# Attention and a dequantized feed-forward layer on one core: the first and last microseconds rearranged, and the turning of the probabilities moved one unit further ahead

## The chip, the cores and the metric

The kernel runs on one core of one Trainium2 chip. The metric is the device time in microseconds (us); three runs give a median of 1543.86 (1541.33 to 1545.67). TensorE is written PE here, VectorE DVE, ScalarE ACT, GpSimd POOL and SyncE SP.

## The reference

x has 16 sequences of 256 tokens and 256 features, all in 32-bit floats. Two sub-layers follow, each with a layer norm (no weights) ahead of it and another behind it, and a residual sum:

```python
q = einsum('bpd,hde->bphe', x, W_Q) + b_Q          # 16 heads of 128; k and v likewise
scores = einsum('bqhe,bkhe->bhqk', q, k) / sqrt(128)
scores = where(causal, scores, -100000.0)
z = einsum('bkhe,bhqk->bqhe', v, softmax(scores))
attn = einsum('bqhe,hed->bqd', z, W_O) + b_O
...
gate, up = xt @ Wg.T, xt @ Wu.T                     # 2048 columns, from 4-bit codes and scales per 32
ffn = (gelu_tanh(gate) * up) @ Wd.T
...
x = x + layernorm(attn(layernorm(x)))
x = x + layernorm(ffn(layernorm(x)))
```

## The kernel before

**Precision.** A 32-bit operand is split into a high part and a rest, and a product is three passes of PE (`mm3`, line 353): high times high, low times high, high times low. Nearly everything outside PE turns results into such pairs: ACT writes the high part out of PSUM, DVE or POOL subtracts it to get the low part.

**Order of work.** The program is one long list. `run` (line 95, issuing in line 99, which is why nearly every row of the profile says L99) records each operation behind the last one of its engine, and `dma` (line 86, rows L88 and L91) does the same for SP, which issues all DMAs. So each engine works in the order in which Python calls these. Background work (layer norms, weight splits, dequantizing) is a generator in a lane (`urgent`, `behind`, `splits`, `idle`, `made`, `spare`); `slot(kinds, ...)` lets one lane take one step at a fixed place of the list.

**Attention.** The 4096 tokens are 8 blocks of 512 (two sequences). A *unit* is one block and one head, 128 in all; a *pair* is two heads, 64 in all. One pass i of the main loop (from -4 to N + 1) does, on PE in this order:

- `st_s(i + 3)`: scores of a unit; DVE adds the mask and finds the row minima, ACT takes exponentials and row sums, POOL multiplies by the reciprocals (tile pr);
- `st_qk(i + 4)`: keys (pk) and queries (pq) of the unit after it, ACT and DVE make kh, kl, kr and qh, ql, qr;
- `st_o(p - 1, i % 2)`: half of a pair's output projection (po);
- `st_z(i)`: probabilities times v (pz), then zh on ACT and zl on DVE;
- `st_v(i + 4)`: a quarter of the v product (pv) of two pairs.

The probabilities have to be turned: DVE transposes 32x32 blocks (`st_t(i + 3)`: tr), four DMAs write them to DRAM (`st_w(i + 3)`: hop<-tr), one reads them back rearranged in the next pass (`st_b(i + 2)`: pt<-hop, two buffers), and a pass later ACT and POOL split them (`st_p(i + 1)`: ph, pl). SP gets, at the end of a pass, first st_b, then st_w, then the weights.

**Weights.** In the first block each pair's weights are loaded raw, split (`w_split`) and kept in DRAM; later blocks load them back (`w_get`). `weights` asks for wk and wq of pair p + 4 in odd passes, and for wo of pair p and wv of pair p + 4 in even ones. Each of wk, wq, wv, wo has two buffers. At a block's end `mid` turns the projection through DRAM (ohop), adds and normalizes, and turns the tokens again (xhop), while `ln1` prepares the next block.

**Feed-forward weights** are dequantized meanwhile in 24 pieces (`f_make` on DVE, then `f_scale` on POOL and ACT), from the last pair of the first block on; small tiles (sg, t, v: tag "code") rotate over four buffers. `f_load` fetches a piece's codes and scales (ld).

**Feed-forward part.** 4 superblocks of two blocks, each with 8 groups of 256 columns: `Two` computes gate and up with seven products instead of eight (m1 to m7, tiles pa, pf, pe, pd), DVE and ACT combine them into `inter`, and `st_d` multiplies by wd one group later, into four PSUM banks that hold 512 tokens by 128 features each. At the end of a superblock the result is turned through DRAM (`end`); in the last one it is turned by PE (`end_now`).

**Ends.** `first_tokens` normalizes the first block: two pieces by DVE, two by ACT, with w_split(0, "k") and w_split(0, "q") between; eight transposes by PE (tpx) follow, behind 24 transposes of the identity that do no work (`warm`). `end_now` takes a block of 512 tokens: eight transposes (tpo), layer norm statistics of four pieces, two pieces normalized by ACT and two by DVE (fa), a residual sum for each half and the store.

Of the kernel before, what the change touches and what calls it, by code (L numbers as in the profile page):

```python
# [18 lines left out]
P = 128  # L19
# [3 lines left out]
NG = 8  # L23
# [5 lines left out]
def kernel(  # L29
# [215 lines left out]
    def first_tokens():  # L245

        xs = [x_load(x, 0, hf) for hf in range(2)]
        yield V_
        stats = []
        for hf in range(2):  # L250
            stats.append((yield from ln_stats([xs[hf][:, t, :] for t in range(2)])))
        w_split(0, "k")
        xn = wide("xn")
        nb = ln_shift(*stats[1], 2)
        for t in range(2):
            mv, rs = stats[0]
            run(
                nc.vector.tensor_scalar,
                xn[:, t, :], xs[0][:, t, :], mv[:, t, 0:1], rs[:, t : t + 1], ALU.subtract, ALU.mult,
            )  # L260
        for t in range(2):
            ln_apply_act(xn[:, 2 + t, :], xs[1][:, t, :], nb, stats[1][1], t)
        w_split(0, "q")
        xt = XT[1, 0] = work.tile([P, 2, 2, TB], F32R, tag="xT", name="xT", bufs=4)
        for hf in range(2):
            tp = ps.tile([P, 2, S], F32, tag=("pk", "pq")[hf], name="tpx")
            for kt in range(2):
                for t in range(2):
                    run(
                        nc.tensor.transpose,  # L270
                        tp[:, kt, t * P : (t + 1) * P], xn[:, 2 * hf + t, kt * P : (kt + 1) * P], ident,
                    )
            cols = slice(hf * S, (hf + 1) * S)
            hi, lo = xt[:, 0, :, cols], xt[:, 1, :, cols]
            run(nc.scalar.copy, hi, tp)
            run(nc.vector.tensor_tensor, lo, tp, f(hi), ALU.subtract)
        ready.add((1, 0))
# [20 lines left out]
    def w_split(p, n):  # L298
# [14 lines left out]
        if n in "vo":  # L313
            run(nc.gpsimd.tensor_tensor, wv_[:, 1], raw, f(wv_[:, 0]), ALU.subtract)
        else:
            run(nc.vector.scalar_tensor_tensor, wv_[:, 1], raw, c, f(wv_[:, 0]), ALU.mult, ALU.subtract)
# [36 lines left out]
    def mm3(o, terms, passes=STATIONARY_LAST, start=True, stop=True, shared=False):  # L353

        todo = [(lhs(a), rhs(c)) for lhs, rhs in terms for a, c in passes]
        for i, (lhs, rhs) in enumerate(todo):
            run(
                nc.tensor.matmul, o, lhs, rhs, start=start and i == 0, stop=stop and i == len(todo) - 1, skip_group_check=shared
            )
# [9 lines left out]
    def st_qk(i):  # L369
# [9 lines left out]
        mm3(pk, [(lambda a, kt=kt: wk_[:, a, kt, cols], lambda c, kt=kt: xt[:, c, kt, :]) for kt in range(2)], MOVING_LAST)  # L379
# [10 lines left out]
        mm3(pq, [(lambda a, kt=kt: wq_[:, a, kt, cols], lambda c, kt=kt: xt[:, c, kt, :]) for kt in range(2)], MOVING_LAST)  # L390
# [83 lines left out]
    def st_b(u):  # L474

        pt = work.tile([P, 4, 6, 32], F32, tag="pt", name="pt")
# [111 lines left out]
    LD = {}  # L588

# [8 lines left out]
    def f_make(g, n, then):  # L598
# [4 lines left out]
        def small_tile(dtype, name):  # L603
            return work.tile([P, 2, 256], dtype, tag="code", name=name, bufs=4)

        c = work.tile([P, 2, 256], I32, tag="raw", name="codes", bufs=6)
        sg, t, v = small_tile(BF16, "sg"), small_tile(BF16, "t"), small_tile(BF16, "v")
# [10 lines left out]
        yield V_  # L618
        run(nc.vector.scalar_tensor_tensor, v, c, 0.5, t, ALU.mult, ALU.max)
# [3 lines left out]
        run(nc.vector.scalar_tensor_tensor, v, sg, 1.0, v, ALU.add, ALU.mult)  # L623
        add(made, f_scale(g, n, v, sc), G_)

    def f_scale(g, n, v, sc):
        scb = sc.unsqueeze(1).to_broadcast([P, 2, 256])
        if n == "d":
            full = work.tile([P, 2, 256], F32, tag="raw", name="full", bufs=6)
            w = f_tile(n)  # L630
            run(nc.gpsimd.tensor_tensor, full, v, scb, ALU.mult)
            yield A_
            run(nc.scalar.copy, w[:, 0], full)
            run(nc.gpsimd.tensor_tensor, w[:, 1], full, f(w[:, 0]), ALU.subtract)
        else:

            full = work.tile([P, 8, P], F32, tag="eight", name="full", bufs=1)
            run(nc.gpsimd.tensor_tensor, full[:, 0:4].rearrange("p (k c) n -> p k (c n)", k=2), v, scb, ALU.mult)
            w = f_tile("u")
# [210 lines left out]
    def st_d(k, bb, dh):  # L850
# [17 lines left out]
        if g == NG - 1:  # L868
            if sb < NSB - 1:
                if dh == 0:  # L870
                    ACC[b] = back_tile()
                back(ACC[b], dh, po)
                if dh == 1:
                    add((urgent, behind)[bb], end(b, ACC.pop(b)), N_)
            else:
                if dh == 0:
                    ACC[b] = wide("oT").rearrange("p a b -> p (a b)").rearrange("p (h n) -> p h n", h=2)
                run(nc.scalar.copy, ACC[b][:, dh], po)
                if dh == 1:
                    add(urgent, end_now(b, ACC.pop(b), tags), V_)  # L880
# [16 lines left out]
    def end_now(b, oT, tags):  # L897

        yield V_
        tp = []  # L900
        for hf in range(2):
            tp.append(ps.tile([P, 2, D], F32, tag=tags[hf], name="tpo"))
            for t in range(2):
                for dh in range(2):
                    run(
                        nc.tensor.transpose,
                        tp[hf][:, t, dh * P : (dh + 1) * P], oT[:, dh, (2 * hf + t) * P : (2 * hf + t + 1) * P], ident,
                    )
        o = [tp[t // 2][:, t % 2, :] for t in range(4)]
        mv, rs = yield from ln_stats(o)  # L910
        nb = ln_shift(mv, rs, 4)
        fa = wide("fa")
        for t in range(2):
            ln_apply_act(fa[:, t, :], o[t], nb, rs, t)
        for t in range(2, 4):
            run(
                nc.vector.tensor_scalar,
                fa[:, t, :], o[t], mv[:, t, 0:1], rs[:, t : t + 1], ALU.subtract, ALU.mult,
            )
        for hf in (1, 0):  # L920
            run(nc.vector.tensor_tensor, X1[b][hf], X1[b][hf], fa[:, 2 * hf : 2 * hf + 2, :], ALU.add)
            dma(half(out, b, hf), X1[b][hf])
# [14 lines left out]
    for n in range(24):  # L937
        run(nc.tensor.transpose, warm[:, n % 4, :], ident, ident)
# [13 lines left out]
    for i in range(-4, N + 2):  # L952
        p = i // 2
        odd = i % 2 == 1
        if p >= 0 and not odd and p < len(pairs):
# [3 lines left out]
            if b == 0 and g == 7:  # L959
                pieces = [(fg, n) for fg in range(NG) for n in "gud"]  # L960
                f_load(*pieces[0])
                for m, piece in enumerate(pieces):
# [3 lines left out]
        if 0 <= i + 3 < N:  # L966
            st_s(i + 3)
        slot(V_)
        if i + 4 < N:
            st_qk(i + 4)  # L970
# [3 lines left out]
        if 0 <= i + 3 < N:  # L974
            st_t(i + 3)
# [6 lines left out]
        if i + 4 < N:  # L982
# [3 lines left out]
        if 0 <= i + 2 < N:  # L986
            st_b(i + 2)
        if 0 <= i + 3 < N:
            st_w(i + 3)
        if odd:  # L990
            weights((p + 4, "k"), (p + 4, "q"))
        else:
            weights((p, "o"), (p + 4, "v"))
# [14 lines left out]
    for k in range(NGRP + 1):  # L1008
        sb, g = divmod(k, NG)
        if k < NGRP:  # L1010
            if g == 2 and sb + 1 < NSB:
                while not {(0, 2 * sb + 2), (0, 2 * sb + 3)} <= ready:
                    step(behind)
                add(spare, x_ops(sb + 1), N_)
            if g == NG - 1:
                for b in (2 * sb, 2 * sb + 1):
                    X1[b] = [x_load(x1d, b, hf, ("pr", "tr")[b % 2]) for hf in range(2)]
# [15 lines left out]
        parts(k, "m7", "m3")  # L1033
        st_d(k - 1, 0, 0)
        slot(V_)
        slot(A_ + G_)
        parts(k, "m4")
# [3 lines left out]
    finish(urgent)  # L1041

# [50 lines left out]
```

## Time and profile before

| | us |
|---|---|
| median of three runs | 1543.86 (1541.33 to 1545.67) |
| the profiled execution | 1548.52 |
| its span, first to last instruction | 1546.7 |
| PE busy | 1510.8 (98%) |
| DVE busy | 1178.4 (76%) |
| ACT busy | 1033.0 (67%) |
| POOL busy | 810.1 (52%) |
| DMA, mean | 263 GB/s |

A row of the timeline has the start, the length, the engine, the line, the operation, the tiles (written <- read) and the number of instructions in it; brackets give the idle time before it and what ended that. Matmuls are pipelined and their ends are modelled, so for PE the distance between starts is read, not the length. SPq is SP issuing DMAs. A row of the windows view has the stretch, its length, then for PE, PE's weight loads, DVE, ACT and POOL the busy us and the instructions, then the granted PE clock, the busy share of the DMA engines and GB/s. The chain is the work that ended last, each step followed back to what released it.

### The profile page before, as it was taken

The page shows a single profiled execution, that of the slowest core. Times are in us where ns is not written, and L with a number is a line of the kernel's source. Part 1 is how long each engine was busy: PE and PEld are TensorE (multiplying, and loading weights), DVE is VectorE, ACT ScalarE, POOL GpSimd, SP SyncE. Part 2 cuts the span into 40 slices and gives each one's busy share as a digit, 9 for nine tenths or more (in the row PEclk, how much of TensorE's full clock was granted, in tenths as well). Part 3 has the DMA queues.
Part 4 walks back from the last instruction along what each step waited for, and adds up shares of the span by engine and source line. Part 5 has one row for each costly group of instructions (what it writes and reads, how often), then busy time and mean ns, then how long its engine had stood idle before and what let it go on. Part 6 is the DMA issues. An engine that isn't in the chain of part 4 may idle for free.

```text
span 1546.7 us, 25648 instructions
## 1 busy us (share of the span) xinstructions
PE 1510.8 (98%) x7792; PEld 1281.4 (83%) x7792; DVE 1178.4 (76%) x2944; ACT 1033.0 (67%) x2600; POOL 810.1 (52%) x1017
## 2 busy tenths in 40 slices
PE   8999999999999999999999999989999999999996
PEld 7888888888888888888888888877788878878884
DVE  6875878788788788878777777847777777787765
ACT  6876667767767676676675777656666665665663
POOL 3754669568667767766866866861420330240100
PEclk9999999999999999999999999989999999999999
DMA  8998899989899999899899889975547456655551
GB/s 276 335 310 257 249 303 302 313 293 300 280 293 317 291 310 296 267 326 309 266 315 294 287 281 322 324 238 204 216 179 275 185 220 212 236 192 214 218 195 42
DMA packets 200411, 407.55 MB, mean 263 GB/s; under 512 B 21457, under 2 KB 128465, under 8 KB 189521
## 3 DMA queue, kind: packets, MB, share of 16 engines
q1 hardware_dynamic: 200272, 405.91, 78.6%
q8 instruction: 62, 1.02, 0.3%
q14 instruction: 77, 0.62, 0.1%
HBM read 294.15 MB, written 111.67 MB: 262 GB/s over the span
## 4 chain that ended last, share of the span: by engine, by line
PE 80%; DMA 6%; DVE 5%; ACT 4%; SPq 2%; issue 1%; POOL 0%; DVEq 0%; POOLq 0%; ACTq 0%
PE pd L99 11%; PE po L99 10%; PE pk L99 10%; PE pv L99 10%; PE pq L99 9%; PE pz L99 9%; PE sc L99 8%; PE pa L99 7%; PE pf L99 5%; DVE sum L99 3%; DMA wo<-wo 2%; PE pe L99 2%; SPq L91 2%; ACT inter L99 1%; DMA hop<-tr 1%
## 5 line engine op out<-in xcount | busy, mean ns | idle before, releaser
L99 POOL TENSOR_SCALAR pr<-pr,rc 128x128 f32<-128x128 f32 (+1 forms) x512 | 251.7, 508 | 80.8 <-DVE rc L99 80.8
L99 POOL TENSOR_TENSOR pl<-pt,ph 128x512 fp32r<-128x512 f32 x128 | 165.3, 1291 | 218.3 <-ACT ph L99 211.8
L99 ACT ACTIVATE pr<-sc,mn 128x128 f32<-128x128 f32 (+1 forms) x512 | 208.9, 421 | 83.1 <-DVE mn L99 81.7
L99 DVE CUSTOM_DVE_ANT_0 sc<-sc,mask 128x128 f32<-128x128 f32 (+1 forms) x512 | 180.7, 373 | 63.5 <-PE sc L99 54.7
L99 PE MATMUL pv<-wv,xT 128*128 128x512 f32 x768 | 208.9, 407 | 0.0
L99 PE MATMUL pd<-inter,wd 128*128 128x512 f32 x768 | 199.5, 393 | 5.2 <-ACT inter L99 4.0
L99 PE MATMUL pk<-xT,wk 128*128 128x512 f32 x768 | 201.5, 398 | 1.6 <-ACT wv L99 1.4
L99 PE MATMUL pq<-xT,wq 128*128 128x512 f32 x768 | 196.4, 391 | 0.0
L99 ACT ACTIVATE zh<-pz,bqk 128x512 fp32r<-128x512 f32 x128 | 88.5, 692 | 160.6 <-PE pz L99 160.6
L99 POOL TENSOR_TENSOR rs<-rs,mhalf 128x4 f32<-128x4 f32 (+1 forms) x33 | 35.1, 1065 | 288.5 <-DVE rs L99 287.2
L99 PEld LDWEIGHTS pd<-inter,wd 128*128 128x128 f32 x768 | 142.3, 188 | 42.5 <-DVE inter L99 7.0
L99 PEld LDWEIGHTS pq<-xT,wq 128*128 128x128 f32 x768 | 144.5, 188 | 32.9
L99 PE MATMUL po<-zh,wo 128*128 128x512 f32 x512 | 160.3, 394 | 8.4 <-DMA wo<-wo 8.4
L99 PEld LDWEIGHTS pk<-xT,wk 128*128 128x128 f32 x768 | 136.5, 190 | 25.5 <-ACT xT L99 1.6
L99 PEld LDWEIGHTS pv<-wv,xT 128*128 128x128 f32 x768 | 135.0, 189 | 23.6
L99 DVE SCALAR_TENSOR_TENSOR zl<-pz,bqk,zh 128x512 fp32r<-128x512 f32 x128 | 95.2, 744 | 76.9 <-ACT zh L99 76.7
L99 ACT COPY part<-pa 128x512 f32<-128x512 f32 x192 | 111.9, 586 | 62.4 <-PE pa L99 59.8
L99 ACT CAST inter<-sum 128x512 fp32r<-128x512 f32 x128 | 80.1, 626 | 101.1 <-DVE sum L99 100.9
L99 DVE TENSOR_TENSOR inter<-sum,inter 128x512 fp32r<-128x512 f32 x128 | 92.1, 720 | 58.9 <-ACT inter L99 56.0
L99 DVE STREAM_TRANSPOSE tr<-pr 128x768 f32<-128x768 f32 x128 | 123.3, 963 | 1.1
L99 PEld LDWEIGHTS po<-zh,wo 128*128 128x128 f32 x512 | 96.1, 189 | 31.1 <-DMA wo<-wo 11.5
L99 DVE SCALAR_TENSOR_TENSOR kl<-pk,bqk,kh 128x512 fp32r<-128x512 f32 x128 | 96.0, 750 | 30.3 <-ACT kr L99 27.1
(139 smaller groups left out, 3792.6 us busy)
## 6 DMA issues: line engine op xcount, KB each, us to landing
hop<-tr SPq DMA_DIRECT2D x512, 96.0 KB
pt<-hop SPq DMA_DIRECT2D x128, 384.0 KB
wk<-wk SPq DMA_DIRECT2D x64, 512.0 KB
wq<-wq SPq DMA_DIRECT2D x64, 512.0 KB
wo<-wo SPq DMA_DIRECT2D x64, 512.0 KB
wu<-fu SPq DMA_DIRECT2D x32, 1024.0 KB
wg<-fg SPq DMA_DIRECT2D x32, 1024.0 KB
wv<-wv SPq DMA_DIRECT2D x56, 512.0 KB
```

The lines of the kernel that those rows point to most:

```text
L91: queue[0] = nc.sync.dma_start(dst, src).ins
L99: ins = op(dst, *args, **kw)
```

## The change

Six things are done at once.

1. *First tokens.* DVE normalizes all four pieces; w_split(0, "k") comes after them and w_split(0, "q") after the copies of the turned tokens. The idle transposes are 30 instead of 24, with 3 and 6 more behind the two groups of tpx. The first v weights' low part goes from POOL to DVE.
2. *Order of passes in pk and pq* (`lows_last`): both high parts of the tokens first, their low parts last.
3. *One unit further ahead.* Scores, keys, turning and its store and load (`st_s`, `st_qk`, `st_t`, `st_w`, `st_b`) are called with an index one higher, the loop begins at -5, and pt has three buffers. `st_p`, `st_z`, `st_o` and `st_v` keep their index.
4. *Weights.* wk and wq are asked for in even passes; wo of pair p + 1 and wv of pair p + 5 in odd ones, which is one pass earlier for these two.
5. *Dequantizing.* The first `f_load` comes at pair 6 instead of 7, two passes earlier; `code` has three buffers, and before v is allocated the scaling of the piece before must stand in the list (`unscaled`).
6. *Last tokens.* The last group's m4 comes ahead of st_d(k - 1, 0, 0). `end_now` is gone; `st_last` takes the last group of the last superblock in four halves of 256 tokens: matmuls of 256 columns, copy, transposes, statistics, and the residual in one step of DVE and one of ACT, one half behind the other. The last half is stored in two pieces.

```diff
@@ first_tokens
-        w_split(0, "k")
         xn = wide("xn")
-        nb = ln_shift(*stats[1], 2)
-        for t in range(2):
-            mv, rs = stats[0]
+        for t in range(4):
+            mv, rs = stats[t // 2]
             run(
                 nc.vector.tensor_scalar,
-                xn[:, t, :], xs[0][:, t, :], mv[:, t, 0:1], rs[:, t : t + 1], ALU.subtract, ALU.mult,
+                xn[:, t, :], xs[t // 2][:, t % 2, :], mv[:, t % 2, 0:1], rs[:, t % 2 : t % 2 + 1],
+                ALU.subtract, ALU.mult,
             )
-        for t in range(2):
-            ln_apply_act(xn[:, 2 + t, :], xs[1][:, t, :], nb, stats[1][1], t)
-        w_split(0, "q")
+        w_split(0, "k")
...
+            keep_warm(3 + 3 * hf)
...
+        w_split(0, "q")
         ready.add((1, 0))
@@ mm3
+        if lows_last:
+            todo = [todo[m] for m in (0, 1, 3, 4, 2, 5)]
@@ st_b
-        pt = work.tile([P, 4, 6, 32], F32, tag="pt", name="pt")
+        pt = work.tile([P, 4, 6, 32], F32, tag="pt", name="pt", bufs=3)
@@ f_make
-            return work.tile([P, 2, 256], dtype, tag="code", name=name, bufs=4)
+            return work.tile([P, 2, 256], dtype, tag="code", name=name, bufs=3)
...
+        while unscaled:
+            step(made)
+        v = small_tile(BF16, "v")
         run(nc.vector.scalar_tensor_tensor, v, c, 0.5, t, ALU.mult, ALU.max)
@@ main loop
-    for i in range(-4, N + 2):
+    for i in range(-5, N + 2):
...
-            if b == 0 and g == 7:
+            if b == 0 and g == 6:
                 pieces = [(fg, n) for fg in range(NG) for n in "gud"]
                 f_load(*pieces[0])
+            if b == 0 and g == 7:
...
-        if 0 <= i + 3 < N:
-            st_s(i + 3)
+        if 0 <= i + 4 < N:
+            st_s(i + 4)
         slot(V_)
-        if i + 4 < N:
-            st_qk(i + 4)
+        if i + 5 < N:
+            st_qk(i + 5)
...
-        if 0 <= i + 2 < N:
-            st_b(i + 2)
         if 0 <= i + 3 < N:
-            st_w(i + 3)
+            st_b(i + 3)
+        if 0 <= i + 4 < N:
+            st_w(i + 4)
         if odd:
+            weights((p + 1, "o"), (p + 5, "v"))
+        else:
             weights((p + 4, "k"), (p + 4, "q"))
-        else:
-            weights((p, "o"), (p + 4, "v"))
@@ st_last, in place of end_now
+        count = len(halves)
+        for n in range(count + 2):
+            if n < count:
+                multiply(n, 0)
+            if 0 <= n - 1 < count:
+                turn_and_measure(n - 1)
+            if n < count:
+                multiply(n, 1)
+            if n >= 2:
+                apply(n - 2)
```

In `apply`, DVE computes x1 + o * rs and ACT adds the shift nb to it:

```python
run(nc.vector.scalar_tensor_tensor, x1[:, t, :], os[n][t], rs[:, t : t + 1], x1[:, t, :], ALU.mult, ALU.add)
run(nc.scalar.activation, x1[:, t, :], x1[:, t, :], AF.Identity, bias=nb[:, t : t + 1])
```

## The prediction, made before the run

> **What bounds the kernel now.** I read the page's busy times first, then the list of what TensorE (PE) waited for, then the chain in order of time, then timelines around each wait. The profiled execution took 1548.52 us, 1546.7 of it span and 1.8 around it. The median of the three runs is 1543.86, so the profiled one is 4.7 slow. About 0.3% (4.6 us) is what a measurement of this kernel can tell from no change.
>
> ```profile
> PE   8999999999999999999999999989999999999996
> ...
> PEclk9999999999999999999999999989999999999999
> ```
>
> The first row is PE's busy share in 40 slices, the second its granted clock, both in tenths: full in nearly every slice; only the two ends and the 27th slice of PE (where attention gives way to the feed-forward part) show anything. So nothing is to be had from shorter work on other engines, only from PE's gaps. In the middle one unit of attention costs a constant: the chain names the first key matmul (pk) at 369.55 and 377.38, 7.83 us apart, and so on for most of 128 units. Where the spacing is larger, PE lost the difference.
>
> ```profile
> 825.63 1.40 PE pk L99 x6
> 835.30 2.43 POOL pr L99 x4
> 839.97 6.26 DMA wo<-wo
> 846.27 2.64 PE po L99 x6
> ...
> 853.19 1.40 PE pk L99 x6
> ```
>
> Three units should pass in 23.50 us between 825.63 and 853.19; they took 27.56. The chain leaves PE for a load of wo that was issued at 839.97 and landed at 846.23. The waits of PE name the same culprit:
>
> ```profile
> PE po L99 <- DMA wo<-wo: 8.4, 6, 4.1
> PE pd L99 <- ACT inter L99: 4.0, 4, 1.9
> PE sc L99 <- DVE kl L99: 2.3, 1, 2.3
> ```
>
> The columns are us in total, times, longest. The DMA queue's own timeline says why wo was late: SP issues everything in order, and at a block's boundary it stood for the read back of the turned output.
>
> ```profile
> 835.59 0.34 SPq L91 DMA_DIRECT2D o<-ohop  x1
> ...
> 837.57 0.42 SPq L91 DMA_DIRECT2D pt<-hop  x1
> 838.09 1.84 SPq L91 DMA_DIRECT2D hop<-tr  x4
> 839.97 0.46 SPq L91 DMA_DIRECT2D wo<-wo  x1
> ```
>
> A long gap costs twice. In windows of 3.4 us the granted clock falls to half afterwards (the figure after the busy times):
>
> ```profile
> 10.40:13.80 3.40, 2.93 (x7) 2.38 (x8) 0.92 (x2) 1.00 (x2) 2.51 (x2) 0.50 0.98 374
> ...
> 153.80:157.10 3.30, 3.30 (x11) 2.91 (x12) 2.96 (x11) 0.97 (x5) 2.05 (x2) 0.50 0.46 99
> ...
> 846.70:850.10 3.40, 3.40 (x13) 2.92 (x12) 3.40 (x11) 2.30 (x8) 3.32 (x8) 0.50 0.94 278
> ```
>
> **Part 1, the wo load one unit earlier.** It moves from the end of unit 2p to the end of unit 2p-1; its reader, the output projection, stays. Pieces: pk spacings over 7.83 at wo waits are 1.04 + 0.17 (from 211), 0.58 (353), 1.08 and 0.58 (589, 606) and 4.06 (841), together 7.5 us, half clock included. Each of these waits is under 2.4 us and the new lead is 7.83 more, so all go: **-7.5**. The load now also waits for the previous reader of its buffer, a projection that PE starts 1.4 us before it is done; SP reaches it later anyway (a projection at about 836.2 to 837.6, the wo issue at 839.97). Queued behind it on SP are the v half, then the next pt load; the v half waits for the unit's last v matmul, about 840.0, against an issue at 840.47, so nothing. What is late next: the k and q loads, which trade places with wo and v and now stand behind the boundary's copies. Such a load, issued at 839.97 and landing at 846.23, is first needed three units after unit 2p began (824.6 + 23.5 + 1.15 of scores = 849.2): 3 us of cover.
>
> **Part 2, scores, turning and storing one unit ahead, three pt buffers.** In the steady state PE's order is the same, with other unit numbers; scores still stand one unit behind their keys. pt gets a unit more between its store and its use. It held ScalarE 37 us over 20 times, but no row of PE's waits names pt, so in the middle I cost it at 0; without that cover the bound is -0.7 (at 845 the pt product was due about when PE would have asked for it). At the drain it counts. From the last scores at 1016.60 to the end of the last projection (1042.88 + 2.75 = 1045.63) PE took 29.0 us for: scores 1.15, six projections of 1.36, four pz of 1.09, three feed-forward products of 1.36, together 17.8. So 11.3 are lost, to a wo wait of 4.08 behind hop<-tr, a pz wait of 1.49, and the half clock from 1024.2 to 1027.5 and from 1031.0 to 1037.7. After, the last scores come one unit before this, pz and pv lie behind them, and no hop<-tr stands just before the last wo. What stays is one short turn: pz 1.07, zh 0.6, ph 0.6, pl 1.29 and 0.3 of handovers are 3.9 to the next pz, with 2.45 of PE work in it: 1.2 to 1.8 lost, and perhaps 1.7 for a half clock. I take 3 left: **-8.3** (between -5 and -10).
>
> **Part 3, the first load of feed-forward weights two units earlier.**
>
> ```profile
> 144.89 0.44 SPq L91 DMA_DIRECT2D ld<-in_gp  x1
> ...
> 151.73 0.49 DVE L99 TENSOR_SCALAR codes<-ld 128x256 int32<-128x256 int32 x2 [5.90 <-DMA ld<-in_gp]
> ...
> 153.40 0.38 PE L99 MATMUL sc<-kl,qh 128*128 128x256 f32 x1 [2.29 <-DVE kl L99]
> ```
>
> VectorE stood 5.90 us for it, and the keys' low part was queued behind. The spacings from 143.93 and 155.24 are 3.48 and 0.91 over: **-4.4**. Two units are 15.7 us against a landing after 6.8, so it goes wholly. Against it: the code buffers fall from four to three, so VectorE's first write of v now waits for GpSimd's scaling of the piece before. In the timelines that scaling ended 0.46 us before the next first write once, 5.1 once, 8 or more in the other 21 pieces. I take 0, bounds 0 and +4.4 once.
>
> **Part 4, the start.** Now the first pk starts at 10.87 and six pk take 0.43 each instead of 0.227. After: VectorE normalizes all four pieces by itself, four times 0.365 from 6.27, the last two held by GpSimd's root (6.32 + 0.70), so done at 7.83; the weight split wk (0.69) follows, to 8.5. Eight transposes at 0.11 and three warming ones end by 8.7, the copy (0.52) at 9.4, first pk at about 9.5, at full clock if the warming holds: 1.35 + 1.2 = 2.6 ahead at the end of pq, whose wq split ends at about 10.9, in time. Then a loss: the v matmuls, which filled the time until qr, now follow the second unit's keys, so the first scores wait for qh and qr (0.25 + 0.36 + 0.5): 1.2 idle. The fill is one unit longer, with ScalarE still late in it (0.93 and 1.23 now). Net **-1.4** (bounds +1 and -2.6).
>
> [...]
>
> **Part 5, the end.**
>
> ```profile
> 1533.91 0.59 ACT L99 COPY oT<-pd 128x512 f32<-128x512 f32 x1 [1.67 <-PE pd L99]
> ...
> 1537.48 1.41 DVE L99 BATCH_NORM_STATS2 st<-tpo 128x6 f32<-128x256 f32 x4
> ...
> 1541.67 1.29 DVE L99 TENSOR_TENSOR xs<-xs,fa 128x512 f32<-128x512 f32 x2
> 1542.38 0.97 SPq L91 DMA_DIRECT2D out<-xs  x2
> ```
>
> PE ends group 30 at about 1523.2 in both, and the end stood 23.5 us after it. Now: inter of the last group is still late (cast 0.62 after the product, 1.1 lost, and 0.5 for the low part); then 48 matmuls of 256 columns at 0.12 (5.7) with 16 transposes (1.8) and about 1 of waits for the copies bring the last matmul to about 1532.4. Then two applications of ScalarE stand ahead of the last copies (0.9 + 0.7), transposes 0.45, statistics 0.75 + 0.3 + 0.2, root 0.8, the shift 0.2, two scaled additions and the second bias 0.37 + 0.37 + 0.6, waits of 0.7 between: about 1538.2. From the last addition to the end there were 3.7 us; I take 3.4 for half the bytes. 1541.6 against 1546.7: **-5.1** (bounds -3 and -6.5).
>
> **Sum.** 7.5 + 8.3 + 4.4 + 1.4 + 5.1 = 26.7 off 1548.5 is 1521.8. Against the median, if its 4.7 less is stalls that go here anyway, 1522; if not, 1517. I take **1520**, its own range 1511 to 1528.
>
> **Rivals.**
> - *The wait moves to the next load.* k and q land behind the boundary, or the drain keeps its gap. For: both loads take the place of wo behind o<-ohop. Against: 3 us of cover. If parts 1 and 2 come to nothing but the rest holds: 15.8 back, 1536; half of it 1528.
> - *VectorE is held by GpSimd's scaling* (the slower side). One such stop of 5.9 us cost 4.4; seven of the 23 pieces outweigh the gain of 26.7, nine give 1520 + 39.6 = 1560. For: at block boundaries the scaling started up to 19 us after v was done. Against: only two of 23 pieces had under 6 us of room.
> - *The ends alone.* The stalls in the middle move on, the start's idle eats the start: about -5, 1539 to 1543.
>
> **Chances.** Forecast 0.60; the wait moves 0.20; the ends alone 0.08; VectorE held 0.08; better than 1511 0.04. Faster 0.84, same 0.08, slower 0.08. The range takes the first two: 1511 to 1536.
>
> **What would show it.** Right: no wo row among PE's waits, pk spacing 7.83 throughout, codes with no wait for ld, half-clock windows gone at 154 and 847, first pk near 9.5, last scores to last projection near 25 us with pv and pz in it. Wrong: PE waits for wk, wq or kl at the boundaries; first writes of v that wait for GpSimd; a half clock within the first 20 us.

## The result, and the profile after

The median of four runs fell from 1543.46 us (1541.33 to 1545.67) to **1524.31 us** (1523.61 to 1525.31): a ratio of 0.9876, with a 95% interval of 0.9859 to 0.9893. The profiled execution took 1523.61, with a span of 1521.8 at a granted clock of 0.997; that of before had 1546.7 at 0.991.

Both spans can be cut at the same matmuls. The rows of the table are distances between starts on PE, and the last column is the difference. The last scores are taken at their first product of kh, the last projection at its last matmul. Units are numbered from 0, so the 17th pk is that of unit 16.

| stretch | before | after | us |
|---|---|---|---|
| span's start to the first pk | 10.87 | 8.86 | -2.01 |
| first pk to the 17th (the fill) | 116.88 | 115.47 | -1.41 |
| 17th pk to the 128th (the middle) | 882.18 | 870.02 | -12.16 |
| 128th pk to the last scores | 6.82 | 6.82 | 0 |
| last scores to the last projection (the drain) | 28.49 | 25.66 | -2.83 |
| last projection to the end | 501.45 | 494.99 | -6.46 |

The fourth part of attention that the loop no longer does ahead (one v product 1.36, one z product 1.09, half a projection 1.36: 3.81 us of PE) went from the first 17 units into the drain. Without that move the first two rows together come to 3.81 - 3.42 = +0.4, and the drain to -2.83 - 3.81 = -6.6.

PE's busy share and granted clock in 40 slices, from the page of the changed kernel:

```profile
PE   8999999999999999999999999999999999999997
...
PEclk9999999999999999999999999999999999999999
```

The dip in the 27th slice, where attention gives way to the feed-forward part, has gone, and the last slice went from 6 to 7. The list of PE's waits in the changed kernel (total us, times, longest):

```profile
PE sc L99 <- ACT qr L99: 4.0, 3, 1.9
PE pz L99 <- POOL pl L99: 1.8, 2, 1.3
...
PE pd L99 <- DVE inter L99: 1.4, 5, 0.3
PE pd L99 <- ACT inter L99: 0.9, 2, 0.4
PE po L99 <- DVE zl L99: 0.7, 1, 0.7
PE pe L99 <- DVE sum L99: 0.5, 2, 0.2
```

There is no wo row any more, and no wait of the scores for kl. What is left stands in the fill (qr), in the drain (pl, zl) and in the feed-forward part (inter, sum). The chain around the boundary of blocks that cost 4.06 us before, in order of time:

```profile
837.85 1.39 PE pk L99 x6
...
845.68 1.40 PE pk L99 x6
...
853.52 1.40 PE pk L99 x6
```

Every piece between them is PE's own, and the keys stand 7.83 and 7.84 apart. That holds for all units from the 17th on, but for one spacing of 8.35 at the 17th that both kernels have: 870.02 is the floor of this stretch. SP's timeline at the same boundary shows what stands where wo was:

```profile
829.91 0.78 SPq L91 DMA_DIRECT2D o<-ohop  x1
...
832.55 1.87 SPq L91 DMA_DIRECT2D hop<-tr  x4
834.47 0.46 SPq L91 DMA_DIRECT2D wk<-wk  x1
835.26 0.67 SPq L91 DMA_DIRECT2D wq<-wq  x1
```

The key and query loads took the late place, and nothing waits for them. The first codes are there when VectorE asks, since its row has no wait for ld, and the keys' low part follows on time:

```profile
150.17 0.47 DVE L99 TENSOR_SCALAR codes<-ld 128x256 int32<-128x256 int32 x2
...
151.65 0.75 DVE L99 SCALAR_TENSOR_TENSOR kl<-pk,bqk,kh 128x512 fp32r<-128x512 f32 x1 [0.46 <-ACT kr L99]
```

The half-clock windows of the middle and the drain are gone (the granted clock is 1.00 from 25.2 to 1505.5). One new window stands in the fill (the columns are those of the prediction's rows):

```profile
21.80:25.10 3.30, 3.30 (x10) 2.53 (x9) 2.32 (x11) 2.58 (x10) 0.82 (x2) 0.50 0.86 240
```

### The profile page after: what moved, and what is told of

Its sections match the earlier page's. It is cut to its first block, busy times and chain, and to the rows that moved or that the text cites. A ratio compares the mean times of both kernels' runs of the same rounds, so it can differ in the third digit from the quotient of the medians.

```text
span 1521.8 us, 25780 instructions
## 1 busy us (share of the span) xinstructions
PE 1502.9 (99%) x7831; PEld 1278.0 (84%) x7831; DVE 1173.2 (77%) x2950; ACT 1034.4 (68%) x2606; POOL 809.4 (53%) x1018
## 4 chain that ended last, share of the span: by engine, by line
PE 89%; DVE 5%; ACT 4%; issue 1%; POOL 1%; DMA 0%; POOLq 0%; ACTq 0%; SPq 0%; DVEq 0%
PE pd L99 11%; PE pk L99 11%; PE po L99 11%; PE pv L99 11%; PE pq L99 11%; PE pz L99 10%; PE sc L99 9%; PE pa L99 7%; PE pf L99 5%; DVE sum L99 3%; PE pe L99 2%; ACT inter L99 1%; DVE inter L99 1%; ACT part L99 1%; ACT o L99 1%
## 5 line engine op out<-in xcount | busy, mean ns | idle before, releaser
L99 PE MATMUL pd<-inter,wd 128*128 128x512 f32 (+1 forms) x792 | 199.7, 386 | 2.6 <-DVE inter L99 1.4
```

Of the source, the lines that this page charges most:

```text
L99: ins = op(dst, *args, **kw)
```

## The experiments

Each run is compared with the kernel before on the same chip; the changed kernel's 1524.31 was measured at another time. "Fill", "middle" and "drain" are the stretches of the table, in the run's profiled execution. The median of before was 1543.33, 1543.25, 1543.74 and 1545.15 at the four times. The ratio is an estimate over all runs and differs from the quotient of the medians by up to 0.0011. The first seven runs ask which part took the waits out of the middle, the last five about the two ends.

| run | median (range) | ratio to before, 95% | fill | middle | drain |
|---|---|---|---|---|---|
| wo earlier, alone | 1543.80 (1540.93 to 1547.61) | 1.0003 (0.9991 to 1.0015) | 119.09 | 881.71 | 24.70 |
| deeper, all loads in one pass | 1548.68 (1543.67 to 1553.87) | 1.0032 (1.0017 to 1.0046) | 116.90 | 891.37 | 27.74 |
| all but the depth | 1532.62 (1529.61 to 1536.79) | 0.9928 (0.9911 to 0.9944) | 119.09 | 881.01 | 22.33 |
| ld late | 1527.20 (1526.60 to 1527.78) | 0.9895 (0.9879 to 0.9912) | 115.77 | 873.83 | 25.69 |
| wo earlier, alone, from block 1 | 1538.21 (1535.60 to 1546.82) | 0.9978 (0.9962 to 0.9994) | 117.73 | 875.90 | 22.63 |
| all but wo's move, from block 1 | 1527.25 (1526.58 to 1529.10) | 0.9905 (0.9884 to 0.9926) | 115.45 | 870.02 | 27.89 |
| all but the depth, from block 1 | 1528.24 (1526.11 to 1530.52) | 0.9910 (0.9891 to 0.9929) | 116.92 | 874.38 | 22.57 |
| second loads later | 1523.93 (1523.28 to 1524.56) | 0.9881 (0.9861 to 0.9902) | 114.15 | 870.02 | 25.85 |
| no warming | 1524.66 (1524.63 to 1525.13) | 0.9875 (0.9858 to 0.9891) | 115.58 | 870.02 | 25.69 |
| drain reordered | 1524.60 (1522.53 to 1525.08) | 0.9871 (0.9855 to 0.9886) | 115.68 | 870.02 | 25.78 |
| both ends | 1522.68 (1522.60 to 1523.01) | 0.9861 (0.9846 to 0.9876) | 114.21 | 870.02 | 24.57 |
| loads later, drain held | 1521.64 (1521.33 to 1522.28) | 0.9849 (0.9823 to 0.9875) | 114.17 | 870.02 | 24.36 |

A drain with the shallow loop (before, and the runs "alone" and "all but the depth") has 3.81 us less of PE's work in it.

### wo earlier, alone

On the kernel before; only the places of the loads change:

```diff
         if odd:
-            weights((p + 4, "k"), (p + 4, "q"))
+            weights((p + 1, "o"), (p + 4, "k"), (p + 4, "q"))
         else:
-            weights((p, "o"), (p + 4, "v"))
+            weights((p + 4, "v"),)
```

> The kernel before, with one edit: wo of pair p + 1 is asked for in odd passes, ahead of wk and wq; wv stays in even ones. Theory (the place of the wo load on SP's queue made the stalls): no wo row among PE's waits, the spacing of pk flat at 7.83 except at 128, 144 and 155 (the first load of codes, 4.4 us, stays), the drain without its 4 us wait and its later half clock; about 10 to 12 us off the kernel before, some 1532. Rival (the extra unit of depth did it): the wo waits go, but PE waits for pz or ph at the same boundaries instead, under 4 us off, 1540 or more.

The wo waits went, and the time stayed. Two new things ate the gain. In the first block, where wo is split and not loaded, the split now took the place in ScalarE's list that the second half of the next block's tokens needed: at the 17th unit the spacing was 13.79, with half clock behind it (ScalarE got pk at 135.60 and pq at 138.16, so six products took 2.56 us, where at full clock they take 1.36). That is an effect of this edit, not of the change. And PE waited for the probabilities' split (pz for ph 2.5, for pl 2.2) at the boundaries and in the drain, with a spacing of 10.61 at unit 106. The run therefore says little of wo by itself; the fifth run repairs it.

### Deeper, with all loads in even passes

On the changed kernel:

```diff
-        if odd:
-            weights((p + 1, "o"), (p + 5, "v"))
-        else:
-            weights((p + 4, "k"), (p + 4, "q"))
+        if not odd:
+            weights((p, "o"), (p + 4, "v"), (p + 4, "k"), (p + 4, "q"))
```

> The changed kernel, with wo of pair p and wv of pair p + 4 asked for in even passes again, ahead of wk and wq; the depth stays. Theory: wo waits of PE come back, 7 to 8 us in the middle at the block boundaries and 2 to 4 in the drain, some 1533 to 1536. Rival (depth removes them): no wo waits, within 2 us of the changed kernel, 1524.

Slower than before. The stall of the first block is in this run too (spacing 13.67 at the 17th unit, 5.3 us of the middle), and the wait for wo spread over eleven places:

```profile
PE po L99 <- DMA wo<-wo: 15.0, 11, 2.6
```

The median lead of a wo load (from its issue to the first projection that reads it) fell to 6.2 us, from 9.5 before and 16.9 in the changed kernel. The four loads of a pair stand in one pass here, so this run tests bunching as much as depth. It shows how little slack the place of a load has here, and it doesn't tell what depth is worth.

### All but the depth

On the changed kernel; the indices of st_s, st_qk, st_t, st_b and st_w go back by one, the loop begins at -4, and the loads are as in the first run:

```diff
-    for i in range(-5, N + 2):
+    for i in range(-4, N + 2):
...
-            st_s(i + 4)
+            st_s(i + 3)
...
-            st_qk(i + 5)
+            st_qk(i + 4)
```

> The changed kernel without its extra unit: loop from -4, scores, keys, turning, store and load at their old index; wo of pair p + 1 in odd passes ahead of wk and wq, wv of pair p + 4 in even ones. Both ends, the early load of codes and three pt buffers stay. Theory (in the middle the depth is worth nothing; it costs about 2 us in the fill and gains 2 to 4 in the drain): spacing of pk flat, first scores without the idle time ahead of them, drain 2 to 4 us longer; 1522 to 1528. Rival (depth matters): waits for pz or ph at the boundaries, 1530 or more.

The same stall of the first block as in the first run is in it (spacing 14.09 at the 17th unit), so only its other rows count. PE waited six times for pl, 4.2 us in all; three of these waits (0.86, 0.52 and 0.85) stand in the middle, at spacings of 9.68, 8.77 and 10.09 (units 76, 90, 106). These were the first sign that depth matters in the middle.

### The first ld two passes later

On the changed kernel:

```diff
-            if b == 0 and g == 6:
+            if b == 0 and g == 7:
                 pieces = [(fg, n) for fg in range(NG) for n in "gud"]
                 f_load(*pieces[0])
```

> The changed kernel, with the first load of codes at pair 7 again, in the same pass as its first use. Theory: VectorE stands about 6 us for it, PE loses 4.4 with the half clock after it, near 1528.7. Rival (another effect of the change had already covered it): no difference, 1524.

The two spacings came back (10.15 and 9.33 at units 19 and 20, 3.81 us of middle), with the wait of the scores for kl of 1.7. The median rose by 2.9 and the profiled span by 4.2. The step of the prediction is confirmed, at 3 to 4 us for a forecast of 4.4.

### wo earlier, alone, from the second block on

As the first run, but the first block's splits stay where they were:

```diff
         if odd:
-            weights((p + 4, "k"), (p + 4, "q"))
+            weights(*[(p + 1, "o")][: p + 1 >= NG], (p + 4, "k"), (p + 4, "q"))
         else:
-            weights((p, "o"), (p + 4, "v"))
+            weights(*[(p, "o")][: p < NG], (p + 4, "v"))
```

> The kernel before, with wo of pair p + 1 asked for in odd passes only where it is a plain load (from the second block on); the first block, where wo is split on ScalarE, keeps its places, so the late token split seen near 130 in e1 should be gone. First theory (the place of the wo load is all, depth is worth nothing in the middle): the middle keeps only the codes stall, about 1532. Second theory, from e1 (wo is only the last of two late loads; without depth pt is late at the same boundaries): PE waits for ph or pl, about 5 us at the boundaries in place of 7.5; with 4 us less in the drain about 1537.

Now wo's move by itself gained 5.0 us by the medians, 3.4 by the ratio. In the profiles it took 6.28 out of the middle and 5.86 out of the drain, but the middle still lay 5.88 over its floor: 2.0 at unit 18 for the late ld, 0.65 and 0.45 at units 26 and 44, and 2.92 at unit 106, where PE waited 0.84 for ph and 0.85 for pl. The theory that wo's place is all failed.

### All but wo's move, from the second block on

On the changed kernel; wo of pair p is again asked for in pass 2p, the first block and all else stay as changed:

```diff
         if odd:
-            weights((p + 1, "o"), (p + 5, "v"))
+            weights(*[(p + 1, "o")][: p + 1 < NG], (p + 5, "v"))
         else:
-            weights((p + 4, "k"), (p + 4, "q"))
+            weights(*[(p, "o")][: p >= NG], (p + 4, "k"), (p + 4, "q"))
```

> The changed kernel, with wo of pair p in even passes again from the second block on, ahead of wk and wq; first block, v and depth as changed. Second theory (both loads are late at the boundaries, each needs its own lead): wo waits of 8 us or more, no waits for ph, 1532 to 1540. If depth alone is enough: no wo waits, 1524.

This overturned the second theory too, that wo and the probabilities each need their own lead. The middle stood at its floor of 870.02 with wo in its old place: no wait for wo there. One wait of 2.6 stayed in the drain, with 2.23 us of drain and 2.9 of the median. SP's timeline at the boundary that cost 4.06 before:

```profile
822.64 0.42 SPq L91 DMA_DIRECT2D wv<-wv  x1
823.11 2.78 SPq L91 DMA_DIRECT2D ohop<-oback  x4
827.67 2.66 SPq L91 DMA_DIRECT2D xhop<-xtr  x4
830.50 0.34 SPq L91 DMA_DIRECT2D o<-ohop  x1
...
834.43 0.50 SPq L91 DMA_DIRECT2D wo<-wo  x1
```

The wo load is issued 3.9 us after the read back of the turned output, as before (4.4). But the read back itself comes earlier: from the first ohop to it 7.4 us pass, where before 9.0 did. The four ohop issues take 2.78 and those of xhop 2.66, where before they took 4.00 and 3.73:

```profile
825.56 0.47 SPq L91 DMA_DIRECT2D wk<-wk  x1
826.07 0.48 SPq L91 DMA_DIRECT2D wq<-wq  x1
826.59 4.00 SPq L91 DMA_DIRECT2D ohop<-oback  x4
830.69 3.73 SPq L91 DMA_DIRECT2D xhop<-xtr  x4
```

At this point PE is 2.95 us further on in the new run, and the wo issue 839.97 - 834.43 = 5.5: a gain of 2.6 against a wait of 2.2 here before. One load (wv) stands ahead of ohop where before there were two (wk and wq), but their number doesn't explain it. In the changed kernel two stand there as well, and the issues take still less:

```profile
822.08 0.50 SPq L91 DMA_DIRECT2D wo<-wo  x1
822.68 0.38 SPq L91 DMA_DIRECT2D wv<-wv  x1
823.10 2.47 SPq L91 DMA_DIRECT2D ohop<-oback  x4
827.17 2.01 SPq L91 DMA_DIRECT2D xhop<-xtr  x4
```

What shortens this stretch, the order of the loads or the pt loads that are no longer urgent, was not tried apart.

### All but the depth, from the second block on

As the third run, with the loads of the fifth.

> e3 with the first block's wo as in e5: no extra unit, wo one pass earlier from the second block on, both ends and the early load of codes as changed. First theory: middle flat, fill about 2 us shorter, drain 2 to 4 longer: 1522 to 1525. Second theory: about 5 us of waits for ph and pl at the boundaries besides: 1527 to 1530.

Without the depth the time is 3.9 us higher by the medians, and the middle 4.36 (spacings 9.94 and 9.62 at units 90 and 106). The list of ScalarE's waits in this run has a row that the changed kernel's list does not have at all:

```profile
ACT ph L99 <- DMA pt<-hop: 59.6, 32, 5.8
```

Before it was 37.0 us over 20 times. The chain at unit 106 of this run, on SP, ScalarE and PE:

```profile
831.91 0.41 SPq L91 DMA_DIRECT2D pt<-hop  x1
```

```profile
837.45 0.62 ACT L99 CAST ph<-pt 128x512 fp32r<-128x512 f32 x1 [4.99 <-DMA pt<-hop]
```

```profile
839.47 0.38 PE L99 MATMUL pz<-pl,vh 128*128 128x256 f32 x1 [0.83 <-POOL pl L99]
```

The pt load, itself behind the boundary's copies, lands 5.5 us after its issue; ScalarE stands 4.99 for it, the split on GpSimd follows, and PE's product comes late. A pass more between the load and the split covers all of that. So with the loads of this run the depth is worth some 4 us in the middle. Before, the wait for wo hid part of it. At the boundary that cost 4.06 there, GpSimd's row is:

```profile
844.77 1.27 POOL L99 TENSOR_TENSOR pl<-pt,ph 128x512 fp32r<-128x512 f32 x1 [5.91 <-ACT ph L99]
```

The split ended at 846.04. PE, held by wo, came to its product at 849.14; without that wait it would have come at about 845.5 (an estimate: pk at 841.13, and 4.36 from pk to this product in the changed kernel), so some 0.5 us were hidden there. The 2.92 and 1.79 that this unit lost in the fifth run and in this one are more. Both runs ask for three weights (wo, wk, wq) in the pass ahead of the boundary's copies, and in the fifth run the pt load was issued 2.1 us earlier than before with PE 3.8 further on. A shallow loop with wo early and these loads apart was not tried, so how much of the 4 us is the depth's own stays open.

### The second loads behind the first pass

On the changed kernel; the raw loads and splits of wk, wq (pair 1) and wv (pair 2) leave the head of the program:

```diff
-    for p, n in (2, "v"), (1, "k"), (1, "q"):
-        w_get(p, n)
...
+        if i == -5:
+            for n in (1, "k"), (1, "q"), (2, "v"):
+                w_get(*n)
```

> The changed kernel, with the second half of the second v weights split one pass later (after the first pass, behind wk and wq of pair 1), so that ScalarE does not stand for its raw load ahead of the first exponentials. Theory (that wait of 2.6 us makes PE's idle 2.0 us at 18.1 and the half clock at 21.8): both go, 3.4 us off the changed kernel, near 1521. Rival (ScalarE's own work is what is late there): the idle time stays at 1.5 or more, within 1 us of 1524.3.

In the changed kernel ScalarE stood for a raw wv that nothing needs soon, ahead of the first exponentials and of the second unit's kh and qr, and PE stood for qr:

```profile
15.37 0.63 ACT L99 ACTIVATE wv<-rawv 128x512 fp32r<-128x512 f32 x1 [2.57 <-DMA rawv<-in_wv]
...
19.81 0.51 ACT L99 ACTIVATE qr<-pq,bqs 128x256 f32<-128x256 f32 x1
```

```profile
20.37 0.49 PE L99 MATMUL sc<-kr,qr 128*128 128x128 f32 x2 [1.88 <-ACT qr L99]
```

With the loads later this wait fell to 0.76, the half clock after it went (the next six pk took 1.38 us, where in the changed kernel they took 2.50), and the fill lost 1.32 us. That is four tenths of the 3.4 expected, and by the medians only 0.4 with ranges that overlap, since this run's first pk stood at 9.56 and a half clock appeared in the drain (two po products took 1.00 us at 1010.47, for 0.45 at 1005.50). So one wait ahead of the scores is explained; three more of about 1 us stay. One of these (1.06 at 26.59) the changed kernel doesn't have, so the waits for qr sum to 3.9 us against 4.0: what the fill lost is mostly the half clock.

### No warming

On the changed kernel:

```diff
-    keep_warm(30)
+    keep_warm(1)
...
-            keep_warm(3 + 3 * hf)
```

> The changed kernel with one warming transpose instead of 30, and none behind the two groups of turned tokens. Theory from the rows (transposes alone raised the clock before): the first keys and queries now start at half clock, 12 matmuls 0.43 us apart instead of 0.23, and the first of them stands no earlier than 8.2 us; the end of the first pq is 1.5 to 2.4 us later, the time 1525 to 1527. [...]

PE's timeline of the start:

```profile
6.58 2.23 PE L99 MATMUL tpx<-ident,xn 128*128 128x128 f32 x8 [4.53 <-DVE xn L99]
9.48 2.93 PE L99 MATMUL pk<-xT,wk 128*128 128x512 f32 x6 [0.67 <-ACT xT L99]
12.21 1.62 PE L99 MATMUL pq<-xT,wq 128*128 128x512 f32 x6
```

The same rows of the changed kernel:

```profile
8.86 1.62 PE L99 MATMUL pk<-xT,wk 128*128 128x512 f32 x6
10.32 1.54 PE L99 MATMUL pq<-xT,wq 128*128 128x512 f32 x6
```

Six pk now start over 2.73 us (9.48 to 12.21), where in the changed kernel they took 1.46 (8.86 to 10.32); the six pq behind them took 1.62, at full clock. The changed kernel had it from 4.68, when PE had done nothing but transposes (from 1.56), and they stood 0.21 apart before that and 0.11 after it. The transposes alone had raised the clock. The run leaves out 38 of them (29 and 9).

The time did not follow, though: 1524.66, and the fill was 115.58 against 115.47. The scores of the second unit now waited 0.76 for qr and not 1.88, and there was no half clock behind it (six pk took 1.36 at 22.56). PE had lost 1.3 us ahead of a place where it stands anyway.

### The drain reordered

On the changed kernel, in the pass with the last scores:

```diff
-        slot(G_)
-        slot(G_)
-        if 0 <= i + 4 < N:
+        if i != N - 5:
+            slot(G_)
+            slot(G_)
+        if 0 <= i + 4 < N and i != N - 5:
             st_t(i + 4)
...
         if 0 <= i + 1 < N:
             st_p(i + 1)
+        if i == N - 5:
+            slot(G_)
+            slot(G_)
```

with st_t(i + 4) of that pass ahead of st_p.

> The changed kernel, but in the pass with the last scores POOL's two normalizations (xn) come behind the split of the next probabilities (pl) instead of ahead of it, and DVE's last turning (tr) comes behind zl instead of ahead of it. Theory: what the drain kept is the order of POOL's and DVE's lists, not the length of the turn. PE's waits for pl of 1.28 us and for zl of 0.67 us go, last scores to last projection falls from 25.7 us to about 24.0, and the time from 1524.3 to about 1522.5. Rival: the short turn pz, zh, ph, pl sets the spacing there anyway; the two waits go but as much appears at the next pz or po: 25.2 to 25.7 us, 1523.9 to 1524.7. Second rival: the later tr stores the last probabilities 0.7 us later, and the last pz waits for them: slower than 1524.3.

What it answers to in the changed kernel, on GpSimd, VectorE and PE:

```profile
1006.38 2.45 POOL L99 TENSOR_SCALAR xn<-xs,mv,rs 128x256 f32<-128x256 f32 x2
1008.80 1.26 POOL L99 TENSOR_TENSOR pl<-pt,ph 128x512 fp32r<-128x512 f32 x1
```

```profile
1006.42 0.98 DVE L99 STREAM_TRANSPOSE tr<-pr 128x768 f32<-128x768 f32 x1 [1.19 <-POOL pr L99]
1007.33 0.71 DVE L99 SCALAR_TENSOR_TENSOR zl<-pz,bqk,zh 128x512 fp32r<-128x512 f32 x1
```

```profile
1008.09 0.50 PE L99 MATMUL po<-zl,wo 128*128 128x512 f32 x1 [0.67 <-DVE zl L99]
...
1010.11 0.39 PE L99 MATMUL pz<-pl,vh 128*128 128x256 f32 x1 [1.28 <-POOL pl L99]
```

Both waits went, and a single one of the same size took their place, for zl. On VectorE and PE of this run:

```profile
1011.35 1.30 DVE L99 STREAM_TRANSPOSE xtr<-xn 128x512 f32<-128x512 f32 x2 [2.71 <-POOL xn L99]
1012.58 0.71 DVE L99 SCALAR_TENSOR_TENSOR zl<-pz,bqk,zh 128x512 fp32r<-128x512 f32 x1
```

```profile
1013.43 0.36 PE L99 MATMUL pz<-ph,vh 128*128 128x256 f32 x1 [1.92 <-DVE zl L99]
```

The xn that had been put off held VectorE's turning of it, and zl stood behind that in the list. With half clock after it (three pa products took 1.43 us at 1015.02, for 0.79 at 1024.19) the drain was no shorter: 25.78. The rival's time held (1523.9 to 1524.7) and its drain to 0.1 us, but not for its reason: it is the order of the lists again, one engine further.

### Both ends

The edits of the last run and of the later loads, and the v products of the first four passes one pass earlier:

```diff
-        if 0 <= i + 4 < N:
+        if i < -1:
+            st_v(i + 5)
+        elif 0 <= i < N - 4:
             st_v(i + 4)
```

> The edit of the drain as above, and in the fill the second loads (wk and wq of pair 1, wv of pair 2) behind the first pass as in an earlier run, with the v products of the first four passes taken one pass earlier, so that one stands between the first queries and the first scores. Theory: the start lost what it gained because the scores wait for qr with nothing to do; one v product (1.36 us) covers the wait of 0.99, and no half clock follows. First key product to the 17th falls from 115.5 us (114.2 with the loads moved alone) to about 113; with the drain's 1.7 the time is about 1521. Rival: ScalarE has no room in the fill; the v results that it copies (vh, vr) come a pass sooner as well and hold up qh and qr, so the wait comes back at the next scores: 114 us or more, 1522 to 1523.

The v product took away the first wait for qr (0.99), and a wait of 2.47 came in the pass that no longer had a v product. The fill was 114.21, the same as with the loads moved alone: the rival's case, a bound that is not PE's. The drain was 24.57, with the same wait of 1.92 for zl but no half clock (three pa products took 0.78 at 1012.85).

### Loads later, and the block's end held in the drain

On the changed kernel; the later loads, the last st_t behind zl as above, the slots in their place, and

```diff
         for jobs in lanes or (splits, urgent, behind, made, spare, idle):
+            if jobs is behind and held[0]:
+                continue
...
+        held[0] = N - 5 <= i <= N - 4
```

> The changed kernel, with the second loads of wk, wq and wv behind the first pass as in the earlier run, and in the drain: the lane of the block's end (behind) gets no step in the pass with the last scores and in the one after it, so neither POOL's xn nor DVE's turning of xn (xtr) stands ahead of pl and zl; the last tr comes behind zl. Theory: in the run before, the wait only changed hands (zl stood behind xtr, which stood behind the xn that had been put off), so with both out of the way the waits for pl and zl go together: last scores to last projection 22.5 to 23.3 us instead of 25.7 (24.6 in the run before), no half clock, 1521.0 to 1522.0. Rival: the work that is put off comes back ahead of the next pl or zl, two passes later, with a wait of the same 1.3 to 1.9 us: 24.5 us or more, 1522.5 to 1524.

The best of all: 1521.64 (1521.33 to 1522.28), a ratio of 0.9849 (0.9823 to 0.9875); its range and the changed kernel's (1523.61 to 1525.31) don't meet, but the two were measured at different times. The drain was 24.36, so 1.3 us of the expected 2.4 to 3.2 came. Of the waits there, two of 0.74 and 0.75 for pl and one of 0.26 for zl are left:

```profile
PE pz L99 <- POOL pl L99: 1.5, 2, 0.7
```

One stands behind a scaling of the feed-forward weights on GpSimd, the other behind the two xn, which came back two passes later: half of the rival's case.

## Why the prediction was right, and where its steps were not

The forecast of 1520 (own range 1511 to 1528) was 4.3 us below the median. The middle, the largest term, is right to 0.3 us; the other three are off by +1.7, +1.8 and -1.4, which cancel in part. Term by term, for the profiled pair (24.9 us of span):

| term | forecast | measured |
|---|---|---|
| parts 1 and 3, the middle | -7.5 and -4.4 | -12.16 |
| part 2, the drain | -8.3 (-5 to -10) | -6.6 |
| part 4, the start | -1.4 (+1 to -2.6) | +0.4 |
| part 5, the end | -5.1 (-3 to -6.5) | -6.5 |
| sum | -26.7 | -24.9 |

**From the sum to the median.** The prediction left open whether the 4.7 us by which its profiled execution was slow go anyway (1522) or not (1517), and took a time between. They go: the changed kernel's profiled execution is 0.7 below its median. The kernels whose middle is at its floor vary by 0.4 to 2.6 us from run to run, the others by 4 to 11 (but for the one with the late ld, 1.2); the first had 4 runs each, the others 4 to 23. So before's excess was most likely its waits for loads, larger in one execution than in another.

**Parts 1 and 2 in the middle: right in sum, wrong in cause.** Reading the spacing of pk against its constant gave the middle to 0.3 us. But the 7.5 were put down to wo's earlier place and the depth was costed at 0 (bound -0.7), because no row of PE's waits named pt. The runs say: wo's move alone leaves 2.92 us at unit 106; all but the depth leaves 4.36 in the middle; all but wo's move leaves nothing there. So in the middle the depth, with the loads in their new order, does the work, and wo's move would not have been needed; it is worth 2.9 us by the medians, in the drain. That the two came in one change is luck for this term: by the prediction's account the change without the depth would have had all of the 7.5 too, and it has 4.36 less (how much of this is the depth's and how much the loads' order stays open). The row of ScalarE's waits for pt, 37 us over 20 times, was read and set aside because PE did not wait. At unit 106 the wait for wo hid a lateness of pt of some 0.5 us, about what the bound allows. What the bound left out is that pt did not come earlier by as much as PE did once the waits for wo were gone (2.1 us against 3.8 in the fifth run).

**Part 2, the drain.** The direction and the size were right to 1.7 us. The loss that stays, counted as the prediction counted it (26.0 us from the last scores to the end of the last projection, less 21.6 of work), is 4.4 us and not 3. The larger part has another reason than the short turn that the prediction named: xn on GpSimd stood ahead of pl, and tr ahead of zl (waits of 1.28 and 0.67). The later waits of 0.26 for zl and 0.50 for pl, whose split stood 1.32 for ph, are that turn. No half clock followed (1.00 from 994 to 1027), where the prediction had allowed 1.7 for one. The last three runs moved the waits about and got 1.3 us back.

**Part 3** is confirmed by its own run (3.81 of the middle for 4.4).

**Part 4 failed.** The first pk came earlier even than said (8.86 for 9.5; 9.43 and 9.56 in two of the runs with the same start) and ran at full clock (six products over 1.46 us). In the kernel before, transposes had raised the clock as well:

```profile
1.56 5.38 PE L99 MATMUL warm<-ident 128*128 128x128 f32 x24 [1.56 <-POOL ident masks.py:199]
8.13 1.35 PE L99 MATMUL tpx<-ident,xn 128*128 128x128 f32 x8 [1.18 <-DVE xn L99]
```

Those of the first row start 0.213 us apart up to 6.53, those of the second 0.109 apart from 8.61 to 8.94, with nothing but transposes on PE until then. No run shows what the upper bound of +1 rested on. Without the warming six of the first twelve products ran at half clock (2.73 us), and the part comes to 9.48 + 115.58 - 127.75 + 3.81 = +1.1. The step that failed is "Net -1.4": that 2.6 us gained by the end of pq stay gained. They met a fill that ScalarE holds up, by splits and loads that stand in its list, and came back as waits for qr (0.99, 1.88 and 1.10, where before there were 0.77 and 1.07) and a half-clock window. The run without warming shows it from the other side: PE 1.3 us later, and the fill as long as before. The prediction had named the fill's late ScalarE and not priced it.

**Part 5** was mis-sized by 1.4 us, at the edge of its bounds. Its terms don't add up to the times that it went on with: up to the last matmul they come to 10.1 us (9.7 if the last four transposes are counted once) and not 9.2, and from there to the last addition to 6.3 and not 5.8. By the terms the part would have been about -4, further from what was measured. PE's last matmuls, and the chain's start at group 30's end:

```profile
1506.54 2.51 PE L99 MATMUL pd<-inter,wd 128*128 128x256 f32 x16 [0.22 <-DVE inter L99]
...
1512.97 0.96 PE L99 MATMUL pd<-inter,wd 128*128 128x256 f32 x6
1514.32 0.82 PE L99 MATMUL tpo<-ident,oT 128*128 128x128 f32 x4 [0.40 <-ACT oT L99]
```

From group 30's end (1505.5) the last product ended 8.3 us later, not 9.2, since it waited 0.22 for inter and not 1.6, and the rest took 8.0 for 9.2. From that gain of 7.2 some 0.7 go back ahead of it, where the last group's two runs of pe products start late (0.27 us at 1500.79 and 0.39 at 1501.99, of which 0.22 is listed as a wait for DVE's sum). With m4 earlier, no pd products stand ahead of them any more, which the prediction did not look for.

**The rivals.** The wait did not move to wk and wq (no row of PE names them after the fill). VectorE was not held by GpSimd's scaling: in the two closest pieces the scaling ended 0.46 and 5.15 us ahead of the next first write of v, as before.

## What to carry to other kernels

That an engine doesn't wait for one thing may only mean that it is late already for another: when the first wait is taken away, look for rows of the engines that feed it (here ScalarE's waits for pt, 37.0 us before) and ask what they become when the main engine is on time. A gain at the start is worth nothing until the engine that sets the fill is known. And an operation put off in an in-order list takes with it all that waits for it on the other engines (xn put off held VectorE's xtr for 2.71 us, and zl behind that held PE for 1.92), so moving one goes wrong unless what reads it is moved too.

## What the runs showed of the hardware that was not expected

- A wait on PE of about 2 us can have a half-clock window of 3.41 us behind it (1.88 for qr at 20.37, half clock from 21.75 to 25.16). Whether it comes is not set by the length of the wait alone. The same wait of 1.92 for zl was followed by half clock with the drain reordered (three pa products took 1.43 us) and not with both ends (0.78), and one of 1.28 for pl with the second loads later (two po products took 1.00) and not in the changed kernel (0.54).
- Four ohop issues of 128 KB on SP took from 1.8 to 4.0 us. The number of 512 KB loads just ahead doesn't set it: at the boundary of unit 106 they took 4.00 us behind two (before), 2.47 behind two (changed) and 2.78 behind one (all but wo's move).
- The first pk moved among runs with the same operations ahead of it on PE: 8.86 (changed), 9.43 (both ends) and 9.56 (second loads later), a spread of 0.7 us, half of the 1.4 that the prediction gave the whole start.
